# An LSTM with a feed-forward network: x Wx of the last 24 steps by Strassen's seven products, gates in pairs

## The chip, the core and the metric

The kernel runs on one core of one Trainium2 chip. The metric is device time in microseconds for one execution, the median of three runs. The engines named below are PE (TensorE, matmuls; PEld its weight loads), DVE (VectorE), ACT (ScalarE), POOL (GpSimd) and SP (SyncE, which here only issues DMAs). Each engine takes its instructions from a queue of its own, and semaphores connect the queues.

## The reference

For 32 sequences of 64 steps with 256 features, an LSTM of 256 units is run, and its outputs go through three layers whose weights are signs (+1 or -1, given as bytes 0 and 1). The result is added to x.

```
xW = x @ Wx + b                          # (32, 64, 1024)
step: a = xW_t + h @ Wh
      i, f, o = sigmoid(a[0:256], a[256:512], a[512:768]);  g = tanh(a[768:1024])
      c = f * c + i * g;  h = o * tanh(c)
y = relu(s0 * [h, -h] @ K0) * 2          # K0 (512, 1024)
y = relu(s1 * y @ K1) * 2                # K1 (1024, 1024)
out = x + s2 * y @ K2                    # K2 (1024, 256)
```

## The kernel before

Time is cut into 8 "halves" of 8 steps (`SB // 2`), two of which make a block of 16 steps; a block has 16 x 32 = 512 rows[...]. The 256 units lie as 4 groups of 64 (`HQ`), each group on 32 partitions, so that a matmul with 32 stationary columns (one step's 32 sequences) fills a quarter of the array and four of them, `q` or `k` = 0 to 3, fill it. All these matmuls are fp32, and PE runs each as two instructions.

Before the loop the weights and the first halves of x are loaded (`load_gates`, `load_x`), idle matmuls run (lines 639 to 643), the x products of the first 12 steps (`AHEAD`) are made, and the bias is spread over the partitions by `copy_bias`. POOL works out a few scalars there and nothing later.

Then line 702 loops over the 64 steps. Each step issues, in this order:

- `gates_from_h` (L305): h Wh, added by PE onto what the gate banks already hold. The gates are kept in the order g, i, f, o (`GATES`); the first bank has three of them, the second has o.
- `cell_step`: on ACT the sigmoids and the tanh (L322 to L324), on DVE `kept`, `new`, `c`, on ACT `th` (L332), on DVE `h` and its transpose into `hist` (L339), which is what PE reads in the next step. At its end, `gates_from_x(t + 1)` puts the x part of the next step into the gate banks with two copies on ACT (L316, L317).
- PE work from a generator, `work`: in steps 0 to 20 (`X_STEPS` = 21) x Wx of the steps still to come, afterwards the layers of the three finished blocks (`ffn_block`). The last block has a function of its own, `last_block`, after the loop; it forms its second layer with Strassen's seven products already. `goal` deals the work evenly: (64-12) x 4 = 208 passes over 21 steps. One pass is one `x_part` with two of the four gates, that is four matmuls of 128 columns; two passes go as one `x_part` of 256 columns. Two steps fill a bank, and `evict_x` (L262) adds the bias on DVE and stores it in `xg`.
- small work on DVE and ACT: transposes of a further half of x (`next_x`, `turn_x`, L229), the split of h into two parts for the layers (`split_h`), the making of the sign weights (`make_w0`, `make_w1`, `make_w2`) and, late, the sums of w1 for the last block (`make_sum`). A counter, `load`, counts the wide DVE operations of a step, and most of this work is issued only where it is below two.

The order on each engine is the order in which the code issues, so what is issued after `cell_step` stands behind the cell in the queues of ACT and DVE. Buffers rotate: four banks for x products and layers (`ps_f`), two for the output (`ps_o`), 24 buffers `act`, 28 `xg`.

Of the kernel before, what the change touches and what calls it, by code (L numbers as in the profile page):

```python
# [30 lines left out]
F32 = mybir.dt.float32  # L33
F32R = mybir.dt.float32r
U8 = mybir.dt.uint8
AF = mybir.ActivationFunctionType
# [5 lines left out]
def lstm_ffn(ctx: ExitStack, tc: tile.TileContext, x, cond, wx_d, wh_d, b_d, k0_d, k1_d, k2_d, s0_d, s1_d, s2_d, out):  # L42
# [14 lines left out]

    GATES = (3, 0, 1, 2)

    AHEAD = 12  # L60
    X_STEPS = 21

    FIRST_CHORE = 2
    W2_STEP = 24
    WARM_UP = 8

# [15 lines left out]
    def act(shape, dtype, name):  # L82
        return apool.tile(shape, dtype, tag="act", name=name)
# [33 lines left out]

    def load_gates(t, w_d, slots, engines, chunks=slice(0, 2)):

        w_rows = w_d.rearrange("(p b) g -> p b g", b=2)  # L120
        s0, n, g0 = slots[0], len(slots), GATES[slots[0]]
        if len(engines) == 1:
            halves = [slice(0, P)]
        else:
            halves = [slice(0, P // 2), slice(P // 2, P)]
        for engine, half in zip(engines, halves):
            engine.dma_start(
                out=t[half, chunks, s0 * H : (s0 + n) * H], in_=w_rows[half, chunks, g0 * H : (g0 + n) * H]
            )

# [3 lines left out]
    for k in range(2):  # L134
        load_gates(wx, wx_d, (1, 2), [nc.sync], slice(k, k + 1))
        for slot in (0, 3):
            load_gates(wx, wx_d, (slot,), [nc.scalar], slice(k, k + 1))
    load_x(0, 1, both)
    load_gates(wh, wh_d, (1, 2), both)
    load_gates(wh, wh_d, (0,), [nc.scalar])  # L140
    load_gates(wh, wh_d, (3,), [nc.sync])

# [3 lines left out]
    b_rows = b_d.rearrange("(o g h) -> o g h", o=1, g=4)  # L146
    nc.gpsimd.dma_start(out=b_row[0][:1, :1], in_=b_rows[:, 3:])
    nc.gpsimd.dma_start(out=b_row[0][:1, 1:], in_=b_rows[:, :1])
    nc.gpsimd.dma_start(out=b_row[1][:1], in_=b_rows[:, 1:3])
    scales = []  # L150
# [58 lines left out]

    def make_w1(k):  # L210
        nc.scalar.activation(w1[:, k, :], bits[k], AF.Identity, bias=nsgn[1], scale=sgn2[1])  # L211
        load_bits(4 + k)

# [22 lines left out]

    load = [0]

# [19 lines left out]
    def evict_x(p, t):  # L258
        xg[t] = gpool.tile([P, 2, 4 * HQ], F32, tag="xg", name=f"xg{t}")
        b = bias.rearrange("p g j -> p (g j)").unsqueeze(1).to_broadcast([P, 2, 4 * HQ])  # L260
        load[0] += 1
        nc.vector.tensor_tensor(xg[t], p.rearrange("p t g j -> p t (g j)"), b, ALU.add)  # L262

    def next_x(half):

        if half < 2 * NB:
            load[0] += 1
            turn_x(*divmod(half, 2))
            if half + 4 < 2 * NB:
                load_x(*divmod(half + 4, 2), [nc.sync])  # L270

    def x_products(t0, t1):

        for t in range(t0, t1, 2):
            p = x_bank(t)
            for s in range(2):
                for k in range(2):
                    start = s == 0 and k == 0
                    passes = min(left_over[0], 2)
                    if passes == 1:  # L280
                        x_part(p, t + s, k, slice(0, 2), start)
                        yield 1
                        x_part(p, t + s, k, slice(2, 4), False)
                    else:
                        x_part(p, t + s, k, slice(0, 4), start)
                    if s == 1 and k == 1:
                        evict_x(p, t)
                        half, left = divmod(t + 2, SB // 2)
                        if left == 2 and half + 1 < 2 * NB:
                            turns.append(half + 1)  # L290
                        if left == 6 and turns:
                            next_x(turns.popleft())
                    yield passes


    hist, hparts = {}, {}

    gate_banks = [ps_g.tile([P, TB], F32, tag=f"gates{n}", name=f"gates{n}") for n in (3, 1)]
    gates = [g[:, : n * HQ].rearrange("p (g j) -> p g j", j=HQ) for g, n in zip(gate_banks, (3, 1))]

    def gates_from_h(t, hT):
        for g, slots in zip(gates, (slice(0, 3), slice(3, 4))):
            for k in range(2):
                for q in range(NQ):
                    nc.tensor.matmul(  # L305
                        g[q * N : (q + 1) * N],
                        hT[:, k, :],
                        wh_q[:, k, q, slots],
                        start=False,
                        stop=(k == 1),  # L310
                        skip_group_check=True,
                    )

    def gates_from_x(t):
        x_t = xg[t // 2 * 2][:, t % 2].rearrange("p (g j) -> p g j", g=4)
        nc.scalar.copy(gates[0], x_t[:, :3])  # L316
        nc.scalar.copy(gates[1], x_t[:, 3:])  # L317

    def cell_step(t, c):
        sig = cell.tile([P, 3, HQ], F32, tag="sig", name=f"sig{t}")  # L320
        cand = cell.tile([P, HQ], F32, tag="cand", name=f"cand{t}")
        nc.scalar.activation(sig[:, 0:2, :], gates[0][:, 1:3], AF.Sigmoid)  # L322
        nc.scalar.activation(cand, gates[0][:, 0], AF.Tanh)  # L323
        nc.scalar.activation(sig[:, 2, :], gates[1][:, 0], AF.Sigmoid)  # L324
# [33 lines left out]
    def evict(p, name):  # L358
        hi, lo = (act([P, TB], F32R, f"{name}{s}") for s in "hl")
        load[0] += 1  # L360
        nc.scalar.activation(hi, p, AF.Relu)
        nc.vector.scalar_tensor_tensor(lo, p, 0.0, hi, ALU.max, ALU.subtract)  # L362
        return hi, lo
# [276 lines left out]
    for g in gate_banks:  # L640
        nc.tensor.matmul(g, idle[:, :P], idle, start=True, stop=True)  # L641
    for n in range(WARM_UP):
        nc.tensor.matmul(p_idle, idle[:, :P], idle, start=True, stop=True)  # L643
# [10 lines left out]
    def copy_bias():  # L654
        p_bias = ps_o.tile([P, 4, HQ], F32, tag="po", name="p_bias")
        for q in range(NQ):
            for i, t in enumerate(b_row):
                nc.tensor.matmul(  # L658
                    p_bias[q * N : (q + 1) * N, 2 * i : 2 * i + 2],
                    first,  # L660
                    t.rearrange("p g (q j) -> p q g j", q=NQ)[:, q],
                    start=(i == 0),
                    stop=True,
                    skip_group_check=True,
                )
        nc.vector.tensor_copy(bias, p_bias)

    banks = [x_bank(t) for t in range(0, SB // 2, 2)]
    for slots in (slice(1, 3), slice(0, 4, 3)):
        for t in range(SB // 2):  # L670
            x_part(banks[t // 2], t, 0, slots, t % 2 == 0 and slots.start == 1)
    copy_bias()
    for t in range(SB // 2):
        x_part(banks[t // 2], t, 1, slice(0, 4), False)
        if t % 2:
            evict_x(banks[t // 2], t - 1)
            if t == 1:
                turn_x(0, 1)
# [13 lines left out]
    chores += [lambda k=k, h=h: make_w0(k, h) for k in range(2) for h in range(2)]  # L692
    chores += [lambda k=k: make_w1(k) for k in range(FC0)]
    chores2 = deque(lambda k=k, m=m: make_w2(k, m) for k in range(2) for m in range(2))
    sum_parts = deque(lambda s=s, k=k: make_sum(s, k) for k in range(K2) for s in range(1, 5))
    splits, w0_parts = deque(), deque()

    work = x_products(AHEAD, T)
    total_x = (T - AHEAD) * 4
    total_ffn = (NB - 1) * (4 * FC0 + 2 * FC0 * FC1 + 4 * FC1)  # L700
    done = 0
    for t in range(T):
        load[0] = 0
        gates_from_h(t, hT)
# [3 lines left out]
        if outputs:  # L708
            load[0] += 1
            if next(outputs[0], "end") == "end":  # L710
                outputs.popleft()
        if t == X_STEPS:
            work, done = ffn(), 0
        goal = (t + 1) * total_x // X_STEPS if t < X_STEPS else (t + 1 - X_STEPS) * total_ffn // (T - X_STEPS)
        while done < goal:
            left_over[0] = goal - done
            done += next(work)
        if t == X_STEPS - 1:
            next(work, None)

        if turns and load[0] < 2:
            next_x(turns.popleft())
        if splits and (load[0] < 2 or t >= X_STEPS or t == SH * splits[0] + 2 * SH - 1):
            split_h(splits.popleft())
        else:
            if t >= FIRST_CHORE and chores:
                part = chores.popleft()()
                if part is not None:
                    w0_parts.append(part)
            elif t >= W2_STEP and chores2:  # L730
                chores2.popleft()()
            if w0_parts and (load[0] < 2 or t == X_STEPS - 1):
                w0_parts.popleft()()
            if sum_parts and t >= SUM_STEP and load[0] < 2:
                sum_parts.popleft()()
    assert not sum_parts
# [31 lines left out]
```

## Time and profile before

| | us |
|---|---|
| median of 3 runs (range) | 312.76 (312.57 to 313.25) |
| the profiled execution | 312.31 |
| its span on the core | 310.5 |
| PE / DVE / ACT / POOL busy | 304.5 / 178.1 / 142.0 / 6.6 |
| before the loop, 0 to 16.8 | 16.84 |
| x stage of the loop, 16.84 to 81.10 (21 steps) | 64.26, of which PE 64.26, DVE 46.60, ACT 37.81 |
| FFN part of the loop and end, 81.10 to 310.5 | 229.4 |

Times come from one execution taken by the profiler; "busy" is the time in which an engine has an instruction under way. A line number such as L305 is the line in the code. In a group or timeline row, `out<-in` names the tiles without buffer numbers, and the arrow in brackets names what an engine waited for. The chain of waits goes back from the last instruction to what released each one, so a long unbroken stretch of PE in it means that PE alone sets the time there. The granted TensorE clock was 0.998 of full speed over the span.

### The profile page before, as it was taken

Reading aid. Unit: us, or ns where it says so; the run is one execution under the profiler, and the core shown is the slowest. Engines: PE = TensorE matmul, PEld = TensorE weight load, DVE = VectorE, ACT = ScalarE, POOL = GpSimd, SP = SyncE. Lnnn points to the kernel's source line nnn. Section 1 sums busy time; section 2 is a strip of 40 time slices with the busy share of each in tenths; the row PEclk is TensorE's granted clock in tenths of the full one; section 3 lists DMA queues with packets and bytes.
Section 4 is the critical chain, followed back from the end, with each engine's and each line's share of the span. In section 5 each row is a group of like instructions: output and inputs, shape, how many; then the busy total and the mean of one; then the engine's idle time right before and its main releaser. Section 6 shows DMA issues by size and latency. Waiting matters only on the chain.

```text
span 310.5 us, 9798 instructions
## 1 busy us (share of the span) xinstructions
PE 304.5 (98%) x4138; PEld 242.7 (78%) x4138; DVE 178.1 (57%) x530; ACT 142.0 (46%) x512; POOL 6.6 (2%) x24
## 2 busy tenths in 40 slices
PE   8999999999999999999999999999999999999994
PEld 4888888788777777777777777777777777899993
DVE  2566767777673444355754445567554434698543
ACT  0225566774564543435633434355443333886220
POOL 5300000000000000000000000000000000000000
PEclk9999999999999999999999999999999999999999
DMA  6874001142000000000010000000310000131002
GB/s 192 206 196 99 5 19 38 36 95 65 3 2 0 2 2 0 3 2 0 2 38 22 14 3 0 2 2 13 92 34 2 3 0 2 31 79 27 2 0 69
DMA packets 30587, 10.89 MB, mean 35 GB/s; under 512 B 27720, under 2 KB 29768, under 8 KB 30544
## 3 DMA queue, kind: packets, MB, share of 16 engines
q1 hardware_dynamic: 27136, 8.66, 11.2%
q10 hardware_dynamic: 3168, 1.57, 2.0%
q8 instruction: 32, 0.52, 0.7%
q0 software_dynamic: 240, 0.04, 0.1%
q14 instruction: 11, 0.09, 0.1%
HBM read 8.16 MB, written 2.10 MB: 33 GB/s over the span
## 4 chain that ended last, share of the span: by engine, by line
PE 97%; DVE 1%; ACT 0%; issue 0%; ACTq 0%
PE p L617 30%; PE gates L305 20%; PE px L246 18%; PE p L591 8%; PE po L604 7%; PE gates L452 4%; PE po L561 2%; PE r L452 2%; PE x L452 2%; PE p L479 2%; PE p_idle L643 1%; PE gates L641 0%; DVE a_7l L362 0%; DVE o L388 0%; PE p_bias L658 0%
## 5 line engine op out<-in xcount | busy, mean ns | idle before, releaser
L305 PEld LDWEIGHTS gates<-wh,hist 128*32 128x32 f32 x2016 | 54.6, 109 | 22.3 <-issue 13.4
L305 PE MATMUL gates<-wh,hist 128*32 128x192 f32 x2016 | 68.1, 275 | 0.0
L246 PE MATMUL px<-wx,xT 128*32 128x256 f32 (+1 forms) x1168 | 60.5, 353 | 0.1
L322 ACT ACTIVATE sig<-gates 128x128 f32<-128x128 f32 x64 | 17.7, 277 | 80.6 <-PE gates L305 80.4
L246 PEld LDWEIGHTS px<-wx,xT 128*32 128x32 f32 x1168 | 42.4, 110 | 11.3 <-DVE c_first L652 0.7
L326 DVE TENSOR_TENSOR kept<-sig,c 128x64 f32<-128x64 f32 x63 | 14.2, 225 | 50.0 <-ACT sig L322 49.7
L332 ACT ACTIVATE th<-c 128x64 f32<-128x64 f32 x64 | 16.4, 257 | 31.4 <-DVE c L330 31.4
L334 DVE TENSOR_TENSOR h<-sig,th 128x64 f32<-128x64 f32 x64 | 14.4, 225 | 20.7 <-ACT th L332 20.7
L262 DVE TENSOR_TENSOR xg<-px,bias 128x512 f32<-128x512 f32 x32 | 21.2, 671 | 2.8 <-PE px L246 2.3
L316 ACT COPY gates<-xg 128x192 f32<-128x192 f32 x64 | 20.0, 313 | 1.3 <-DVE xg L262 1.3
L591 PE MATMUL p<-hhi,w 128*128 128x512 f32 x48 | 19.3, 402 | 0.0
L591 PE MATMUL p<-hlo,w 128*128 128x512 f32 x48 | 19.1, 398 | 0.0
L339 DVE STREAM_TRANSPOSE hist<-h 128x64 f32<-128x64 f32 x64 | 15.7, 245 | 2.4
L330 DVE TENSOR_TENSOR c<-kept,new 128x64 f32<-128x64 f32 x64 | 14.4, 224 | 2.2
L324 ACT ACTIVATE sig<-gates 128x64 f32<-128x64 f32 x64 | 14.9, 233 | 0.1
L323 ACT ACTIVATE cand<-gates 128x64 f32<-128x64 f32 x64 | 14.0, 218 | 0.0
L328 DVE TENSOR_TENSOR new<-sig,cand 128x64 f32<-128x64 f32 x64 | 13.9, 217 | 0.0
L317 ACT COPY gates<-xg 128x64 f32<-128x64 f32 x64 | 13.0, 203 | 0.0
L591 PEld LDWEIGHTS p<-hhi,w 128*128 128x128 f32 x48 | 9.0, 188 | 2.2
L591 PEld LDWEIGHTS p<-hlo,w 128*128 128x128 f32 x48 | 9.0, 188 | 2.0
L211 ACT ACTIVATE w<-bits,nsgn,sgn 128x1024 fp32r<-128x1024 uint8 x8 | 9.9, 1241 | 0.0
L617 PE MATMUL p<-a_7h,w 128*128 128x512 f32 x24 | 9.9, 413 | 0.0
(249 smaller groups left out, 602.8 us busy)
## 6 DMA issues: line engine op xcount, KB each, us to landing
x<-in_x_dram SPq DMA_DIRECT2D x60, 64.0 KB, 2.8
out_dram<-o SPq DMA_DIRECT2D x28, 64.0 KB, 1.8
bits<-in_L_ffn_k_dram SPq DMA_DIRECT2D x10, 128.0 KB, 3.2
wx<-in_L_cond_Wx_dram SPq DMA_DIRECT2D x2, 256.0 KB, 4.2
wx<-in_L_cond_Wx_dram ACTq DMA_DIRECT2D x4, 128.0 KB, 4.6
wh<-in_L_cond_Wh_dram ACTq DMA_DIRECT2D x2, 256.0 KB, 5.6
wh<-in_L_cond_Wh_dram SPq DMA_DIRECT2D x2, 256.0 KB, 6.2
k<-in_L_ffn_k_dram SPq DMA_DIRECT2D x2, 256.0 KB, 3.1
```

Source lines behind the costliest of these rows:

```text
L246: nc.tensor.matmul(p[q * N : (q + 1) * N, t % 2, slots], xT[i // 2, i % 2][:, s, k, :], wx_q[:, k, q, slots], start=start, stop=False, ski ...
L262: nc.vector.tensor_tensor(xg[t], p.rearrange("p t g j -> p t (g j)"), b, ALU.add)
L305: nc.tensor.matmul(g[q * N : (q + 1) * N], hT[:, k, :], wh_q[:, k, q, slots], start=False, stop=(k == 1), skip_group_check=True,)
L316: nc.scalar.copy(gates[0], x_t[:, :3])
L322: nc.scalar.activation(sig[:, 0:2, :], gates[0][:, 1:3], AF.Sigmoid)
L324: nc.scalar.activation(sig[:, 2, :], gates[1][:, 0], AF.Sigmoid)
L332: nc.scalar.activation(th, c, AF.Tanh)
L339: nc.vector.transpose(hT, h.rearrange("p (j b) -> p b j", b=2))
L452: nc.tensor.matmul(bank[pair][:, i], a(k)[:, ts(2 * pair + i, P)], b(k, n), start=first and i == 0 and k == 0 and n == 0, stop=last and k ...
L591: nc.tensor.matmul(p, w0[:, k, ts(m, P)], a[:, k, :], start=(n == 0), stop=(n == 3))
L604: nc.tensor.matmul(po[m], w2[:, m, k], a1[k][n], start=(k == 0 and n == 0), stop=(k == FC1 - 1 and n == 1))
L617: nc.tensor.matmul(p1[m], w1[:, k, ts(m, P)], a0[k][n], start=(k == 0 and n == 0), stop=(k == FC0 - 1 and n == 1),)
```

## The change

**Seven products.** For halves 5, 6 and 7 (`FIRST_QUARTERS` = 5, so the last 24 steps) x Wx is made by Strassen's scheme (its form with 15 additions). A half's x is cut into four quarters: two feature chunks by two groups of four steps; Wx into four: two chunks by two pairs of gates. Seven products of quarters take the place of eight; each is 16 matmuls of 128 columns, four passes. `sum_wx` forms the four sums of Wx on POOL, once, before the loop. `differ_x` forms the four differences of x on DVE for each half, in two pairs. `x_products_of(i, n)` issues product n of half i. It uses three banks: x (products 1, 2), q (a copy of product 1 on ACT, then 6, 5, 3 added) and r (the bias copied in on ACT, then 7, 4 added). Products 6 and 5 are followed by a copy of q to SBUF on ACT (`uv`), and four `take_x` on DVE per half add the bias or a `uv` and store the result.

**Order.** `QUARTERS` gives the products of steps 9 to 19, mostly two a step. `X_STEPS` is 20. The ordinary products now end at step 40 of the sequence and fill the rest of each step's goal: 112 + 84 = 196 passes over 20 steps.

**Gates in pairs.** The gates are kept as i, f, o, g, two to a bank; the weights are loaded by pairs, so that each load has fewer and longer pieces, and the bias in two loads.

**Room.** `load` counts columns instead of operations (512, 360 for a pair of differences or an output part, 320 for a split), with `ROOM` = 1100, and `copies` counts the extra ACT operations of a step. w1 is made in halves. Two banks are zeroed before the loop, with two idle matmuls fewer.

```diff
-    X_STEPS = 21
+    X_STEPS = 20
+    FIRST_QUARTERS = 5
+    QUARTERS = [
+        [(5, 1), (5, 7)], [(5, 2), (5, 6)], [(5, 5), (6, 1)], [(5, 3), (5, 4)], [(6, 7), (6, 6)], [(6, 2), (6, 5)],
+        [(7, 1), (6, 3)], [(6, 4), (7, 7)], [(7, 6), (7, 2)], [(7, 5)], [(7, 3), (7, 4)],
+    ]
-    WARM_UP = 8
+    WARM_UP = 6
...
     def next_x(half):
         if half < 2 * NB:
-            load[0] += 1
+            load[0] += 512
             turn_x(*divmod(half, 2))
+            if half >= FIRST_QUARTERS:
+                differences.extend((half, ns) for ns in ((1, 3), (2, 4)))
...
+    def differ_x(i, ns):
+        if i not in x_sum:
+            x_sum[i] = act([P, 4, SB // 4, N], F32, f"tx{i}")
+        t = x_sum[i]
+        b11, b12, b21, b22 = (x_quarter(i, k, half) for k in range(2) for half in range(2))
+        load[0] += 360
+        for n in ns:
+            in0, in1 = {1: (b12, b11), 2: (b22, t[:, 0]), 3: (b22, b12), 4: (b21, t[:, 1])}[n]
+            nc.vector.tensor_tensor(t[:, n - 1], in0, in1, ALU.subtract)
...
+    def x_products_of(i, n):
...
+        if n == 1:
+            x = banks["x"] = quarter_bank(ps_f, "pf", f"qx{i}")
+            turns.append(i + 1)
+        if n == 7:
+            r = banks["r"] = quarter_bank(ps_f, "pf", f"qr{i}")
+            copies[0] += 1
+            nc.scalar.copy(flat(r), bias_of(1))
...
+        for s in range(SB // 4):
+            for k in range(NQ):
+                nc.tensor.matmul(p[k * N : (k + 1) * N, s], b[:, s], w[:, k], ...
+        if n == 1:
+            q = banks["q"] = quarter_bank(ps_o, "po", f"qq{i}")
+            copies[0] += 1
+            nc.scalar.copy(q, x)
+        elif n == 2:
+            take_x(i, 0, 0, x, bias_of(0))
+        elif n in (6, 5):
+            t = uv[i, n] = act([P, SB // 4, 2, HQ], F32, f"uv{i}_{n}")
+            copies[0] += 1
+            nc.scalar.copy(t, q)
+            if n == 5:
+                take_x(i, 1, 1, r, flat(t))
+        elif n == 3:
+            take_x(i, 0, 1, q, bias_of(0))
+        elif n == 4:
+            take_x(i, 1, 0, r, flat(uv[i, 6]))
...
-        nc.scalar.activation(sig[:, 0:2, :], gates[0][:, 1:3], AF.Sigmoid)
-        nc.scalar.activation(cand, gates[0][:, 0], AF.Tanh)
+        nc.scalar.activation(sig[:, 0:2, :], gates[0], AF.Sigmoid)
+        nc.scalar.activation(cand, gates[1][:, 1], AF.Tanh)
...
     for t in range(T):
...
+        if t == X_STEPS - len(QUARTERS) - 2:
+            turns.append(FIRST_QUARTERS)
+        if X_STEPS - len(QUARTERS) <= t < X_STEPS:
+            for i, n in QUARTERS[t - X_STEPS + len(QUARTERS)]:
+                while turns and turns[0] <= i:
+                    next_x(turns.popleft())
+                while differences and differences[0][0] <= i and n > 2:
+                    differ_x(*differences.popleft())
+                x_products_of(i, n)
+                done += 4
         while done < goal:
             left_over[0] = goal - done
             done += next(work)
...
-        if turns and load[0] < 2:
+        if w0_parts and load[0] + 512 <= ROOM:
+            load[0] += 512
+            w0_parts.popleft()()
+        if turns and load[0] + 512 <= ROOM:
             next_x(turns.popleft())
+        if differences and load[0] + 360 <= ROOM:
+            differ_x(*differences.popleft())
```

## The prediction

> **What bounds the kernel now.** I read the page's busy shares first, then the chain of waits in order of time, then the timeline of one step. PE is busy for 304.5 of 310.5 us, and the chain gives it 97% of the span, so time is the sum of what PE does plus every moment it is made to wait. The chain of waits (start us, length us, work) shows what one step costs, here step 9 (from 44.00) to step 11 and two steps of the later FFN part:
>
> ```profile
> 44.00 0.87 PE gates L305 x32
> 44.87 2.16 PE px L246 x48
> 47.03 0.87 PE gates L305 x32
> 47.91 1.95 PE px L246 x40
> 49.85 0.93 PE gates L305 x32
> 50.78 2.16 PE px L246 x40
> ...
> 97.08 1.01 PE gates L305 x32
> 98.09 3.17 PE p L617 x13
> 101.26 1.01 PE gates L305 x32
> 102.27 3.40 PE p L617 x14
> ```
>
> A step is 0.87 us of gates and, for ten "passes" of x Wx (a pass: four 128-column matmuls, two instructions each), 2.16 us. Steps with 128- and 256-column instructions mixed (x48) and with 256 alone (x40) both take 2.16, so a pass costs 0.216 us in either width; nine take 1.95.
>
> The second thing to see is how close the recurrence runs. The timeline of the same step (start, length, engine, line, operation):
>
> ```profile
> 44.77 0.28 ACT L322 ACTIVATE sig<-gates 128x128 f32<-128x128 f32 x1 [0.28 <-PE gates L305]
> 45.73 0.26 ACT L332 ACTIVATE th<-c 128x64 f32<-128x64 f32 x1 [0.46 <-DVE c L330]
> 45.89 0.31 ACT L316 COPY gates<-xg 128x192 f32<-128x192 f32 x1
> 46.14 0.20 ACT L317 COPY gates<-xg 128x64 f32<-128x64 f32 x1
> 46.28 0.24 DVE L339 STREAM_TRANSPOSE hist<-h 128x64 f32<-128x64 f32 x1
> 46.28 1.25 ACT L211 ACTIVATE w<-bits,nsgn,sgn 128x1024 fp32r<-128x1024 uint8 x1
> 46.45 0.68 DVE L262 TENSOR_TENSOR xg<-px,bias 128x512 f32<-128x512 f32 x1
> 47.05 0.71 DVE L229 STREAM_TRANSPOSE xT<-x 128x512 f32<-128x512 f32 x1
> ```
>
> Counted from the gates' start at 44.00, ACT is free for other work only at 2.28 and DVE only at 2.45: whatever the code issues after `cell_step` stands behind the cell in these queues. It costs nothing today because PE never needs it in the same step: this xT is used a step or more later. In the nine-pass step `hist` ends at 49.55 (49.31+0.24) and the gates take 0.93 instead of 0.87, as if they started at 49.91: from a DVE result to PE I count 0.36 us, and use it for ACT results too. From a product's end to a copy of it on ACT I take 0.12 (gates of 192 columns end at 44.00+0.65, `sig` starts at 44.77).
>
> **What goes.** Three eighths-of-x (halves 5 to 7) need 7x4=28 passes instead of 32: 12 passes x 0.216 = **-2.6 us**. A step now has 196/20=9.8 passes, before 208/21=9.9.
>
> **What moves.** Step 20 becomes an FFN step. There gates cost 1.01, and 3.17 less 13 x 0.23 (3.40-3.17) leaves 0.18 for the switch: 1.19 against 0.87, **+0.3**. Same FFN work in 44 steps. Gates as 128+128 instead of 192+64 have the same columns (0.87), but `cand` waits for the second bank, ending at 0.87 instead of 0.65; it started 0.17 behind `sig` before, so it comes 0.05 later. Ten-pass steps (3.03) cover that; a nine-pass step, which the recurrence holds at 2.88 now, goes to 2.93, and three such unstalled steps instead of two make **+0.2**.
>
> **What is added on PE's path.** I replayed the loop's counters by hand. With ROOM 1100 and 512 for an eviction or a transpose, two of them fill a step. Half 5 enters `turns` in step 7, which has an eviction and xT4; step 8 has two evictions; so its transpose is forced inside step 9, immediately before product (5,1), and both pairs of differences before (5,7). The same happens to xT6 (step 11: w0's last part takes the room of step 10), to the differences of 6 (step 13), xT7 (15), and the differences of 7 (16). And each product 7 needs the bias copied into its bank by a copy issued just ahead of it on ACT. All of these stand behind the cell of their own step, PE takes its products in order, and the one or two filler passes come after the row. Nothing covers the wait. Durations: a transpose 0.70 (L229 mean), an eviction or take 0.65 to 0.67 (L262), a 512-wide ACT copy 0.59 out of PSUM (L482 mean 592) and 0.55 estimated for the bias from the 192- and 64-wide copies (313, 203); a 128-wide subtraction 0.29, between the rows of 64 (225) and 256 (414). Two operations of one queue overlap by about 0.05 (46.45+0.68 against 47.05). The cell's new tail adds 0.05. From the gates' start:
>
> - Step 9, (5,1): DVE free 2.50, xT5 ends 3.20, PE at 3.56 instead of 0.87: **2.7**. It ends 4.43; q copy from 4.55, bias copy ends 5.64, (5,7) at 6.00: **1.6** (the four differences, 3.15 to about 4.2, lie beneath it).
> - Step 11, (6,1): (5,5) ends 1.73; its copy on ACT 2.33 to 2.92, take(1,1) on DVE to 3.61, xT6 behind it to 4.25, PE at 4.61 instead of 1.73: **2.9**.
> - Step 13, (6,7): second difference (product 7's) ends 3.03, bias copy 2.88 beneath it, PE at 3.40 instead of 0.87: **2.5**.
> - Step 15, (7,1): as (5,1), **2.7**.
> - Step 16, (7,7): take(1,0) to 3.15, two differences to 3.63, PE at 3.99 instead of 1.73: **2.3**.
>
> Together **+14.7 us**. In the other rows each product's source comes from an earlier step (q's copies and uv are a row apart in `QUARTERS`), so I charge nothing there; in steps 10, 14 and 17 a uv copy and half of w1 follow the last product on ACT and may hold the next cell by 0.1 each.
>
> Bounds. 0.36 as the latency to PE could be 0.15 (the 49.55 to 49.67 gap to the first weight load is 0.12): six waits, -1.3. If a difference's reader waits for all four, 0.5 more in steps 13 and 16: +1.0. Late cells: +0.5. So +13.4 to +16.2 for the waits.
>
> **What is hidden.** Four takes per half replace four evictions, equal size. Twelve 0.6 us copies on ACT and twelve 0.29 us differences fit: ACT is busy 37.8 and DVE 46.6 of the x stage's 64.3 us. w1 in halves: 0.72 each (L215, 128x512 from bytes, 715) instead of 1.24, +0.2 on ACT in the queue's tail, its last half ready in step 19 and first used in step 22. In the FFN part the room rule moves sums and outputs by a few steps, on queues with slack (there the cell needs 2.9 of 4.1 us). The start has as many idle matmuls (2+2+6 for 2+8) and 16 bias matmuls as before; wx's second pair comes in one 256 KB transfer per chunk on ACT's queue in place of two of 128 KB, and wh in four transfers on the same two queues: the px group that waited 0.12 us ("issue" at 7.39) may gain or lose that. The new work on POOL has no near row (its widest operation is 128x1, 0.19). The Trainium skill, "GPSIMD Engine Reference", section "Elementwise — side-by-side cycle accounting", gives 4497 ns for 2048 columns: my estimate for 512 is 1.1 to 1.3 us, so the four sums run from 11.4 (POOL's last operation today) to about 16.6; first use is after 44. Even a DVE operation held up by one of them would cost 1.3 once, before step 0.
>
> **A rule against the change.** The granted clock is 0.998 and the trace has no PE gap over 0.4 us from the first matmul to 260 us, so it can't show what repeated gaps do. The Trainium skill, "TensorE: Matmul & The Clock Gate", section "Why this matters for your kernels", warns of idle gaps above about 3 us, after which PE falls to half its clock. The largest gap here is 2.9. By the row (full clock): nothing. By the rule, if gaps this near do trip it, the 2.2 us of work behind each of five stalled steps doubles: up to +11. I take nothing: no gap is past the bound, and each stalled step also has 3 us of work.
>
> **Sum.** -2.6 +0.3 +0.2 +14.7 = +12.6. The profiled run took 312.31 (span 310.5 and 1.8 around it): 324.9. The median shown is 0.45 higher: **325.3 us**.
>
> **Rivals.**
> - Only the bias copies wait (my replay of the room is wrong and transposes and differences run a step early, as their queue `differences` is meant to allow). Then (5,7) waits to 2.33+0.54+0.55+0.36=3.78, 2.05; (6,7) 2.37; (7,7) 1.5: 5.9-2.1 gives 316.5. For: w0's parts decide step 10 by one unit. Against: the replay reproduces DVE's order in today's trace. 8%.
> - No wait binds, and it is not slower: the copies, turns and differences land before PE asks. Price -2.1, 310.7. It decides as soon as six waits sum to less than 2.1, 0.35 each: that needs them to run ahead of the cell, against the order in the rows above. 7%.
> - The clock falls in the gaps: +5 to +11, 330 to 336. 9%.
> - The likeliest, 324 to 328 by its bounds, 325.3: 76%.
>
> The range is 320 to 332: it takes in a few waits smaller or missing, and half of the clock's case. A difference under 0.2% can't be told from none here. Faster 0.06, same 0.02, slower 0.92.
>
> **What will show it.** In the changed profile: steps 9, 11, 13, 15, 16 of 5.3 to 7.3 us, the others 2.9 to 3.1; PE waits for DVE `xT` three times (2.7 to 2.9 each), for `tx` twice (2.3 to 2.5), for the bias copy once (1.6); x stage ending near 92.5 instead of 81.1; granted clock still 0.99 in it. I am wrong if PE shows no such gaps in steps 9 to 16, or if matmuls after gaps run at half speed.

## The result and the profile after

| | before | after |
|---|---|---|
| median (range), us | 312.78 (312.57 to 313.25) | 332.86 (328.63 to 333.7) |
| ratio | 1 | 1.0601 (1.0565 to 1.0637), that is +18.8 us |
| profiled execution / span | 312.31 / 310.5 | 332.36 / 330.6 |
| x stage of the loop, to the end of the gates that follow it | 16.84 to 81.10 (21 steps) | 16.93 to 99.78 (20 steps) |
| PE / DVE / ACT / POOL busy | 304.5 / 178.1 / 142.0 / 6.6 | 311.3 / 185.0 / 155.9 / 11.1 |

The ratio leaves out the slowest of the four runs after, 333.7, and lies below that of the medians, 1.064. The change made the kernel 6% slower. The forecast of 325.3 had the direction and the place right, but was 6 to 8 us short. The chain of waits around step 9 (gates from 43.84; start, length, work; `...` marks rows left out):

```profile
45.82 0.27 ACT th L441
46.08 0.02 issue
46.11 0.24 DVE h L443
46.34 0.02 issue
46.37 0.04 DVE hist L448
...
46.54 0.72 DVE xT L229
47.27 0.14 issue
47.40 1.93 PE qx L370 x32
49.34 1.23 issue
50.57 1.93 PE qr L370 x32
52.50 0.85 PE px L248 x8
53.36 1.21 PE gates L410 x32
54.56 0.87 PE qx L370 x32
55.44 0.87 PE qq L370 x32
```

Before, this chain was PE alone. Now it leaves PE, goes through the whole cell and through the transpose xT behind it, and only then comes back: product (5,1) starts at 47.40, in place of right behind the gates. The second thing to see is in the lengths. `qx` and `qr`, right after the gaps, take 1.93 us for the same 32 matmuls that take 0.87 a step later (54.56, 55.44), the filler takes 0.85 in place of 0.43, and even the next gates are slow.

What PE waited for, in total, times and longest (the waits of PE itself):

```profile
PE qx L370 <- DVE xT L229: 7.8, 3, 2.8
PE qr L370 <- DVE tx L328: 2.2, 1, 2.2
PE qr L370 <- ACT w L210: 1.9, 1, 1.9
...
PE qr L370 <- issue: 1.2, 1, 1.2
```

Six waits, the six of the forecast, in steps 9 (two), 11, 13, 15 and 16. The last row is (5,7), whose bias copy ends at 50.47, 0.1 before it starts. The third is (7,7), which reads no `w`: its difference ends at 88.10, 0.15 before it, and the `w` happened to end later. And the stages from step 9 on (stretch: length, PE busy, weight loads, DVE, ACT, POOL, then the granted clock, DMA share and GB/s):

```profile
43.90:53.36 9.46, 5.75 (x115) 4.68 (x110) 3.68 (x12) 3.14 (x10) 0.00 (x0) 0.67 0.05 16
53.36:63.92 10.56, 7.78 (x222) 7.43 (x217) 4.74 (x14) 4.84 (x17) 0.00 (x0) 0.82 0.07 16
63.92:74.09 10.17, 7.96 (x232) 7.72 (x227) 5.14 (x18) 4.99 (x17) 0.00 (x0) 0.84 0.30 67
74.09:84.39 10.30, 7.80 (x223) 7.56 (x219) 4.82 (x15) 4.44 (x16) 0.00 (x0) 0.83 0.01 2
84.39:89.76 5.37, 3.44 (x112) 3.08 (x108) 3.25 (x12) 2.50 (x8) 0.00 (x0) 0.98 0.01 3
```

PE is busy for 32.73 of 45.86 us, so it idles for 13.1; and the granted clock, 1.00 throughout the same stage of the kernel before, is 0.67 to 0.84 in the first four stretches. The spread of the runs belongs to this: the run of 328.63 had a mean clock of 0.988, those of 332.36 and 333.35 had 0.974.

### The profile page after: what moved, and what is told of

Its sections match the earlier page's. It is cut to its first block, busy times and chain, and to the rows that moved or that the text cites. A ratio compares the mean times of both kernels' runs of the same rounds, so it can differ in the third digit from the quotient of the medians.

```text
span 330.6 us, 10413 instructions
## 1 busy us (share of the span) xinstructions
PE 311.3 (94%) x4426; PEld 253.0 (77%) x4426; DVE 185.0 (56%) x542; ACT 155.9 (47%) x532; POOL 11.1 (3%) x27
## 4 chain that ended last, share of the span: by engine, by line
PE 91%; ACT 3%; DVE 3%; issue 1%; DVEq 0%; ACTq 0%
PE p L726 28%; PE gates L410 18%; PE px L248 10%; PE p L700 7%; PE po L713 7%; PE gates L561 3%; PE qx L370 2%; PE qq L370 2%; PE po L670 2%; PE r L561 2%; PE x L561 2%; PE p L588 2%; PE qr L370 2%; ACT w L210 1%; PE p_idle L756 1%
## 5 line engine op out<-in xcount | busy, mean ns | idle before, releaser
L410 PE MATMUL gates<-wh,hist 128*32 128x128 f32 x2016 | 69.3, 278 | 0.0
L410 PEld LDWEIGHTS gates<-wh,hist 128*32 128x32 f32 x2016 | 55.0, 111 | 17.0 <-issue 13.1
L248 PE MATMUL px<-wx,xT 128*32 128x256 f32 (+1 forms) x784 | 41.2, 352 | 0.0
L248 PEld LDWEIGHTS px<-wx,xT 128*32 128x32 f32 x784 | 29.1, 115 | 6.6 <-DVE c_first L765 0.8
L426 ACT COPY gates<-xg 128x128 f32<-128x128 f32 x80 | 18.1, 258 | 1.7 <-DVE xg L264 1.7
L432 ACT ACTIVATE cand<-gates 128x64 f32<-128x64 f32 x64 | 14.3, 223 | 9.0 <-PE gates L410 8.9
L437 DVE TENSOR_TENSOR new<-sig,cand 128x64 f32<-128x64 f32 x64 | 14.3, 223 | 7.1 <-ACT cand L432 6.5
L264 DVE TENSOR_TENSOR xg<-px,bias 128x512 f32<-128x512 f32 x20 | 13.2, 671 | 5.6 <-PE px L248 5.4
L370 PE MATMUL qx<-wx,xT 128*32 128x128 f32 x192 | 8.6, 333 | 7.8 <-DVE xT L229 7.8
L433 ACT ACTIVATE sig<-gates 128x64 f32<-128x64 f32 x64 | 14.0, 219 | 0.1
L370 PEld LDWEIGHTS qx<-wx,xT 128*32 128x32 f32 x192 | 6.9, 132 | 8.5 <-issue 8.5
L210 ACT ACTIVATE w<-bits,nsgn,sgn 128x512 fp32r<-128x512 uint8 x16 | 12.5, 808 | 0.0
L426 ACT COPY gates<-xq 128x128 f32<-128x128 f32 x48 | 10.8, 258 | 0.0
```

Of the source, the lines that this page charges most:

```text
L210: nc.scalar.activation(w1[:, k, cols], bits[k][:, cols], AF.Identity, bias=nsgn[1], scale=sgn2[1])
L248: nc.tensor.matmul(p[q * N : (q + 1) * N, t % 2, slots], xT[i // 2, i % 2][:, s, k, :], wx_q[:, k, q, slots], start=start, stop=False, ski ...
L370: nc.tensor.matmul(p[k * N : (k + 1) * N, s], b[:, s], w[:, k], start=(n == 1 and s == 0), stop=(n in (2, 3, 4)), skip_group_check=True,)
L410: nc.tensor.matmul(g[q * N : (q + 1) * N], hT[:, k, :], wh_q[:, k, q, ts(i, 2)], start=False, stop=(k == 1), skip_group_check=True,)
L426: nc.scalar.copy(g, x_t)
```

## The experiments

The theory after the traces: 13.1 us are waits for work that stands behind the cell of its own step, and the clock falls in the gaps these waits make. Its rivals: the products are slow, or lower the clock, by their own form; and, for the waits, that only the bias copies or only DVE's part count.

**Is the clock lowered by the gaps?** The first try put idle matmuls of zeros before the products that wait:

```diff
+                for _ in range(FILL.get((i, n), 0)):
+                    nc.tensor.matmul(
+                        gate_banks[0][:, 2 * HQ :], idle[:, :P], idle[:, : TB - 2 * HQ],
+                        start=False, stop=True, skip_group_check=True,
+                    )
                 x_products_of(i, n)
```

> The changed kernel with all its waits, but 69 idle matmuls (384 columns of bf16 zeros, about 0.16 us each, into an unused part of a gate bank) put before the six products that wait, somewhat less than each gap. Theory (PE's idle gaps drop the clock): the granted clock stays at 0.98 or more in steps 9 to 16, products take 0.87 again, and the time is the changed kernel's less about 8.6, 323 to 325. Rival (the clock is lowered by the load or form of the products, not by the gaps): products after a gap still 1.5 to 1.9 us, time 331 to 334.

Measured: 329.42, ratio 1.0527 (1.0513 to 1.0542), clock 1.00. The clock held, but the time missed the theory's range: the idle matmuls shared a bank with the gates, waited for ACT's gate copies (5.3 us in five waits) and ended after the gaps that they were to fill. In step 9 the transpose is through at 47.53 there, and the idle matmuls run from 46.57 to 48.84. So it was done again into bank x, which waits for nothing:

```diff
+        for _ in range(FILL.get((i, n), 0)):
+            nc.tensor.matmul(
+                flat(x).rearrange("p t c -> p (t c)"), idle[:, :P], idle,
+                start=(n == 1), stop=True, skip_group_check=True,
+            )
         for s in range(SB // 4):
```

> The idle fill again, with 512-column idle matmuls (0.22 us each) into bank x of the same half, which nothing holds at that time, so that they run inside the gaps: 10, 11, 9, 10 and 8 of them before (5,1), (6,1), (6,7), (7,1), (7,7); (5,7) keeps its gap of 1.2. Theory (idle gaps drop the clock): clock 0.99 or more in steps 9 to 16, products 0.87 to 1.1, the waits as long as in the changed kernel, time 323 to 325. Rival (the form of the products lowers the clock): 331 to 334.

Measured: 325.34, ratio 1.0404 (1.0387 to 1.0422), just above the theory's range of 323 to 325, far from the rival's. Step 9, and the stalled product of step 13, in its chain of waits:

```profile
47.24 0.72 DVE xT L230
...
48.01 1.08 PE qx L376 x32
49.09 1.24 issue
50.33 1.08 PE qr L376 x32
51.41 0.43 PE px L249 x8
51.84 0.87 PE gates L416 x32
...
66.34 0.39 DVE tx L329 x2
66.73 0.14 issue
66.86 1.08 PE qr L376 x32
```

The same transpose is still waited for, the same gap of 1.24 is there, but no product takes 1.93. With work that computes nothing the kernel is 6.7 us faster (spans 330.6 and 323.9), though this run came to its step 9 0.7 us later: steps 9 to 16 take 45.7 and 38.2, so the clock cost 7.5 us there. A first product after a wait still takes 1.08 instead of 0.87, so a wait costs 0.2 beyond its length.

**Do gaps do it without any of the products?** In the kernel before, a matmul of zeros that reads a tile filled by DVE behind the cell:

```diff
+        if t in (9, 11, 13, 15, 17):
+            for _ in range(1):
+                nc.vector.memset(dz, 0.0)
+            nc.tensor.matmul(
+                gate_banks[0][:N, 4 * HQ : 6 * HQ], dz[:, :N], dz[:, P : 2 * P],
+                start=False, stop=True, skip_group_check=True,
+            )
```

In the longer one the loop runs twice.

> The kernel before with a wait of PE put into steps 9, 11, 13, 15 and 17: one matmul of zeros after the gates that reads a tile which DVE fills behind the cell. Gaps of about 2.2 us. If gaps alone drop the clock at this size: clock below 0.9 in these steps, 327 to 334; if it holds: 312.8 + 11 = 324, clock 0.99.

> The same with the tile filled twice, gaps of about 2.7 us, as the longest of the changed kernel. Theory (gaps drop the clock): the work after each gap at half speed for some 3 us, 312.8 + 13.4 + 8 = 334, clock near 0.8 in these steps; rival (only the seven products' form does): 326, clock 0.99.

Measured: 334.6 (ratio 1.0705, 1.0668 to 1.0741) with five waits of 2.3, 11.6 us together; 336.45 (1.0764, 1.0742 to 1.0786) with five of 3.0, 14.8 together. Steps 9 to 17, 27.1 us before, take 45.5 and 48.4, which is 6.8 and 6.4 more than the waits. (The rest of each run's difference, 0.5 us ahead of step 9 and 2.6 behind step 17, has another cause, which is open.) Chain of waits of the shorter one around the first, the second and the last gap:

```profile
47.74 0.27 PE gates L716
...
48.12 2.05 PE px L247 x40
...
56.37 0.36 PE gates L716
56.73 3.85 PE px L247 x38
...
87.52 0.27 PE gates L716
87.79 2.25 PE px L247 x38
```

The x products here are the old ones, 256 columns wide. After the first gap and the last they run as ever, but for the 0.2; after the second, of the same size, they take 3.85. So gaps alone halve the speed, but not every gap does: three of five did in either run.

Which ones, the record of the clock tells. It has two values only, 1.00 and 0.50, and in the changed kernel's loop it changes at 47.09, 53.91, 60.74, 64.15, 70.98, 74.39, 81.22 and 84.63, always 3.41 us or twice that apart; where these stretches begin differs from run to run. Here are such stretches of the shorter run (the first four) and of the longer run (the last two), with the columns of the table of stages above:

```profile
53.01:56.42 3.41, 1.10 (x40) 0.94 (x38) 2.57 (x8) 2.35 (x8) 0.00 (x0) 1.00 0.12 38
56.42:59.84 3.42, 3.42 (x37) 2.30 (x41) 1.02 (x2) 0.00 (x0) 0.00 (x0) 0.50 0.00 0
83.73:87.15 3.42, 1.45 (x44) 1.17 (x36) 2.65 (x9) 2.56 (x8) 0.00 (x0) 1.00 0.23 52
87.15:90.56 3.41, 3.04 (x67) 2.37 (x68) 1.07 (x3) 0.00 (x0) 0.00 (x0) 1.00 0.02 5
65.42:68.83 3.41, 1.62 (x48) 1.31 (x37) 2.62 (x9) 2.68 (x9) 0.00 (x0) 1.00 0.12 38
68.83:72.24 3.41, 2.24 (x45) 1.78 (x49) 0.90 (x3) 0.88 (x1) 0.00 (x0) 1.00 0.19 43
```

A gap counts by what falls into one stretch. In the loops of all profiled kernels, a stretch at full clock in which PE was busy for 1.38 us or less was followed by one at half clock, ten times of ten; with 1.45 or more, never. (At the ends of the kernels one with 1.52 still was, so the bound is no sharper than that.) A gap of 3.0 that lies across an edge, as in the last two rows, did nothing; in the changed kernel gaps of 2.2 to 2.8 that lay mostly in one stretch did. PE was busy for 15.1 us at half clock there, which cost half of it, 7.6; in these two runs 9.8 and 9.2, which cost 4.9 and 4.6.

**Are all six waits a matter of order?** Everything that a product needs is issued at the end of an earlier step, by a table:

```diff
+    PLAN = {1: 'w', 2: 'x', 3: 'w', 5: 'x', 6: 'x', 7: 'd', 9: 'dx', 10: 'dw', 11: 'd', 13: 'x', 15: 'd', 16: 'dw'}
...
+        for part in PLAN.get(t, ""):
...
+        if t in (8, 12, 15):
+            prepare_r({8: 5, 12: 6, 15: 7}[t])
```

In the table `w` is a part of w0, `x` a transpose and `d` a pair of differences; `prepare_r` takes bank r and issues its bias copy. To make room, half 5 enters the queue in step 6, and the making of w0 and w1 may begin in step 0 instead of 2.

> The changed kernel with every transpose, difference and bias copy that a product needs issued at the end of an earlier step, same products and rows. Theory (the loss is waits behind the cell of the same step, 13.1 us, and the half clock after them, 8.6 us): no PE wait above 0.4 us in steps 9 to 19, granted clock 0.99 or more there, x stage ending near 79, time 310.5 to 312.5, under the kernel before. Rival (the seven products are slow in themselves, or pull the clock down by their form): products still take more than 0.9 us each and the time stays above 318.

Measured: 312.75, ratio 0.9995 (0.9984 to 1.0006), clock 1.00. The six waits are gone, 20 us come back, and what remains is the kernel before to within 0.1%. The rival's forecast, above 318, is out, but the theory's, 310.5 to 312.5, is missed too: PE has 2.6 us less to do, and nothing came of it. The chain of waits shows where to look:

```profile
58.67 0.87 PE qq L377 x32
59.54 0.17 PE px L249 x2
59.71 0.42 issue
60.14 0.53 PE px L249 x11
```

"issue" in the middle of a group: PE stands still and waits for nothing that the profile shows. From the first gates at 17.46 to those of step 20 at 79.65 the loop takes 62.2 us. At the pace of the kernel before (nine ten-pass steps from 52.94 to 80.23, 0.216 a pass) its twenty gates and 196 passes would take 59.8. So 2.4 us are lost, nearly all from step 10 on. PE is idle for 0.46 of them, and 0.35 are the gates after four nine-pass steps (0.95 to 0.97 for 0.87); the rest lies in rows that have become longer.

**Only the bias copies left in place** (the table, without `prepare_r`):

> As the first, but the three bias copies stay where the change has them, just ahead of product 7. Theory: waits only before (5,7) of about 1.8, (6,7) of 2.2 and (7,7) of 1.4, together 5.4 us; 316 to 317 if the clock holds, up to 320 if gaps of this size drop it. Rival (the copies were always hidden, only the transposes and differences counted): 310.5 to 312.5, as the first.

Measured: 316.9, ratio 1.0128 (1.0110 to 1.0147), clock 0.996. Waits of PE 1.7 before (5,7) and 3.3 in the other two (2.1 and 1.2), together 5.0, and the clock stays at 1.00 in the loop. The copies were a wait of their own, worth about 4 us, and the transposes and differences on top of them the rest.

**Is a narrow pass as cheap as a wide one?** The forecast priced a pass at 0.216 in either width. The kernel before with every x_part as two of 128 columns:

```diff
                     else:
-                        x_part(p, t + s, k, slice(0, 4), start)
+                        x_part(p, t + s, k, slice(0, 2), start)
+                        x_part(p, t + s, k, slice(2, 4), False)
```

> The kernel before with every x_part of the loop issued as two of 128 columns in place of one of 256, so the same columns with twice the instructions; nothing else. With everything ahead the seven products still gave nothing: step 13 showed 0.4 us in which PE waited for nothing the profile shows, and x stage was 2.3 us longer than its passes. Theory (narrow instructions are not free: PE runs out of instructions at that rate): 1 to 4 us slower, with idle of PE put down to issue in the x stage. Rival (a pass costs 0.216 in either width, as the mixed steps say): no difference, within 0.3.

Measured: 320.58, ratio 1.0250 (1.0223 to 1.0276): +8 us, twice what the theory allowed, for the same columns and the same sums. Its x stage takes 73.2 us (16.66 to 89.88) in place of 64.26, at a clock of 1.00. Of the 9 us more, PE is idle for 4.5; the others lie in rows that have become longer. The chain of waits late in it:

```profile
76.17 2.18 PE px L246 x80
...
82.34 0.65 PE px L246 x21
82.99 0.56 issue
83.55 1.82 PE px L246 x57
```

A narrow stretch can still run at 27 ns a matmul (2.18 for 80), and then PE stands still, 0.1 to 0.7 us in most steps. A step here has 112 matmuls and 112 weight loads, in 3.44 us: 15.4 ns each. The kernel before has 72 to 80 of each in 3.03. The mixed steps that the forecast leaned on (48 matmuls, 16 of them narrow) were below that rate and could not show it.

What PE waits for shows in another place, the DMA queue that brings instructions (packets, MB, share; the kernel before, then this run):

```profile
q8 instruction: 32, 0.52, 0.7%
q8 instruction: 39, 0.64, 0.9%
```

A packet has 16,384 bytes, and seven more of them came with 1632 more instructions of PE. In this x stage PE starts 256 instructions, on the mean, from one packet to the next. By the trace's times of the single transfers they are 3.9 us apart on the mean here, 3.9 to 6.2 in the kernel before; and each of the 13 standstills of 0.1 us or more ends 1.3 to 1.6 us after a packet has landed. The one in the run with everything ahead, above, ends at 60.14, 1.3 after a packet that landed at 58.80, and the packets are 3.5 to 4.3 apart there from step 9 on. This ties the standstills to the supply of instructions, though no run varies the supply itself. What holds the packets at this spacing is not shown, nor whether matmuls or weight loads alone would do it, as both double here.

**The seven products where they aren't dense.** Halves 6 and 7 alone, mostly one product a step, the rest in wide passes, all ahead:

```diff
-    FIRST_QUARTERS = 5
+    FIRST_QUARTERS = 6
     QUARTERS = [
...
+        [(6, 1)], [(6, 2)], [(6, 6)], [(6, 5)], [(6, 7), (6, 3)], [(6, 4), (7, 1)],
+        [(7, 2)], [(7, 6)], [(7, 5)], [(7, 7), (7, 3)], [(7, 4)],
     ]
```

> Seven products for halves 6 and 7 alone, everything ahead as in the first run, and at most one product a step in eight of eleven steps (three have two), the rest of each step in 256-column passes; take (1,1) follows product 7. 200 passes, ten in each of 20 steps. Theory (narrow instructions cost where they are dense, 0.04 us a pass when all of a step is narrow): steps of 3.05, x stage of 61 us, with the moved step's 1.4 in the FFN part 310.7 to 312.0, a little under the kernel before. Rival (each narrow pass costs the same however it is spread): 312.5 to 313.5.

Measured: 312.26, ratio 0.9990 (0.9977 to 1.0004), between the two forecasts. Steps 10 to 14 take 3.04 to 3.06, and PE is idle for 0.2 us in the whole loop, so the standstill is all but gone where a step has one product, or two now and then. The time is 0.3 under the kernel before, not clear of it.

**The two remaining terms.** X_STEPS 20 in the kernel before, nothing else:

> The kernel before with X_STEPS 20 in place of 21 and nothing else: 10.4 passes a step. It measures the moved step alone. By the prediction's sum +0.3; by the traces (FFN part 1.4 longer, gates of the x stage 0.87 shorter) +0.5: 312.9 to 313.4. If fuller steps hide the recurrence better it is the same as before.

Measured: 312.99, ratio 1.0012 (0.9999 to 1.0024), +0.4 us, not quite clear of none. And the pairing of the gates alone:

> The kernel before with the gates in pairs alone (order i, f, o, g, two to a bank, loads by pairs), without the seven products and without the new room rule. Theory: cand starts 0.05 later, which only nine-pass steps show: +0.1 us, and the start shifts by no more than 0.2: 312.6 to 313.2, no difference that can be told. Rival (the pairing lengthens every step or the start): 315 or more.

Measured: 312.8, ratio 1.0001 (0.9992 to 1.0009). It costs nothing that can be told from none.

## Why the prediction was right, and where it was short

- **Direction and place: right, shown.** The loss sits in steps 9, 11, 13, 15 and 16, before the six products named, for the reason given: their transposes, differences and bias copies are issued behind the cell of the same step. Moving them ahead takes the whole loss away.
- **Size of the waits: right, 14.7 forecast, 14.3 measured.** The forecast's 0.36 from a DVE result to PE was counted to where a product would have started if it took its usual 0.87. The second filled run shows both halves of it in step 13: 0.14 from the difference to PE, then 1.08 for the product, together 1.22, against 0.36 + 0.87 = 1.23. So PE's idle time, 13.1, and the six longer first products, 0.2 each or 1.2, belong together. One by one: 2.7, 3.0 and 2.7 before qx for 2.7, 2.9 and 2.7; (5,7) 1.4 for 1.6; (6,7) 2.4 for 2.5; (7,7) 2.1 for 2.3.
- **The clock: 0 forecast, 7.6 measured.** This is the step that failed. The row and the rule were weighed, and nothing was taken "because no gap is past the bound, and each stalled step also has 3 us of work". Four gaps of 2.2 to 2.8 us did halve the clock, for 3.4 to 6.8 us each, work in the step or not, and the x stage ended at 99.78 instead of near 92.5. The prediction's own sign of being wrong, matmuls after gaps at half speed, is what the profile shows. The Trainium skill's warning ("TensorE: Matmul & The Clock Gate", section "Why this matters for your kernels") was the right one to heed; its figure of about 3 us is not the bound here, where a gap of 2.2 was enough and one of 3.0 across an edge was not. The third rival, the clock's, priced at 5 to 11 and given 9%, is what came on top.
- **The range held by luck.** By the ratio the result is 331.6, by the medians 332.9, both at the edge of 320 to 332 and far from the likeliest case, 324 to 328 at 76%. It lies where the clock's rival was priced, 330 to 336. How much of a gap falls into one stretch differs from run to run: by its mean clock the run of 328.63 spent about 8 us at half clock and those at 0.974 about 17, by my estimate (2 x 0.012 x 326.7 and 2 x 0.026 x 330.6).
- **A pass costs the same in either width: wrong where narrow work is dense.** It hardly shows in the changed kernel, whose waits left time for the instructions to arrive: steps 17 to 19 take 9.14, as their gates and passes do. But it is why the rival "no wait binds", 310.7, is not what the run with everything ahead gave: the saving of 2.6 us is given back as the 2.4 us that its loop takes longer.
- **The moved step** +0.3, measured 0.4; **the pairs** and **POOL's sums** as said: each sum took 1.28 us, from 11.63 to 16.75, under cover.
- **The rival "only the bias copies"** was priced at 316.5; built, it takes 316.9. That it comes so close is in part luck, since its waits were 5.0 for 5.9.

With the measured terms, and -2.6 and +0.5 (0.3 for the moved step, 0.2 for nine-pass steps) as forecast, the sum is -2.6 +0.5 +13.1 +1.2 +7.6 = +19.8. It belongs to the profiled run, whose span is 20.1 above that of the kernel before; the +18.8 of all runs includes one that lost less to the clock.

## What to carry to other kernels

Before adding work to a step whose engines run a recurrence, ask not whether the engine has room but where in its queue the new work lands: behind the cell means at the end of the step, and whatever PE needs from it must be issued a step earlier. Price a PE gap of about 2 us or more at its length, 0.2 for the first product behind it, and a stretch of half clock (here up to 1.7 us each), and look at the granted clock of the stage first. An algorithm that saves multiplications by halving the width of each instruction saves nothing if the supply of instructions, not the columns, becomes the limit: try the width by itself, at the density of the real step, before building the rest.

## What the runs showed of the hardware that was not expected

The granted clock changed only at the edges of stretches of 3.41 us, and fell to half after a stretch in which PE was busy for less than about 1.4 us: ten times of ten in the loops, where four gaps of 2.3 to 3.0 us that an edge divided did nothing. Idle matmuls of zeros in the gaps kept it at 1.00. In a stage with 112 matmuls and as many weight loads a step, PE fell behind by 0.4 us a step, and its 13 standstills ended 1.3 to 1.6 us after a packet of instructions had landed; with 72 to 80 of them in 3.03 us it showed none.
